# Key projection by seven block products with summed context blocks, in a one-core perceiver block

## The chip, the cores and the metric

The kernel runs on one NeuronCore of a Trainium2 chip. The metric is the device time of one execution in microseconds (us), lower being better; for the kernel before it is 1882.07 us, the median of three runs. A profile is one further execution recorded by the hardware profiler.

The engines are TensorE (PE; its weight loads are shown apart as PEld), VectorE (DVE), ScalarE (ACT), GpSimd (POOL) and SyncE (SP). Each works through its own instructions in the order in which the program issues them and waits for the others by semaphores. SP only issues DMAs here. A matrix product reads its operands from SBUF and writes into one of eight PSUM banks (128 partitions x 512 fp32 each), and DVE or ACT must take the result from there.

## The reference, cut to what matters

```python
def xattn(query, key, value, Wq, Wk, Wv, Wo):      # 32 query heads, 8 key heads of 32
    q = (query @ Wq).reshape(b, sq, 32, 32).transpose(0, 2, 1, 3)
    k = (key @ Wk).reshape(b, sk, 8, 32).transpose(0, 2, 1, 3)
    v = (value @ Wv).reshape(b, sk, 8, 32).transpose(0, 2, 1, 3)
    k, v = repeat(k, 4, axis=1), repeat(v, 4, axis=1)
    probs = softmax(einsum('bhqd,bhkd->bhqk', q, k) * 32 ** -0.5)
    return einsum('bhqk,bhkd->bhqd', probs, v).transpose(0, 2, 1, 3).reshape(b, sq, 1024) @ Wo

x = x + xattn(layernorm(x), ctx_4096, ctx_4096, Wq, Wk, Wv, Wo)
x = x + self_attention_with_rope(layernorm(x), ...)
x = x + quantised_ffn(layernorm(x), ...)
```

`x` is 16 x 64 x 1024, the context 16 x 1024 x 1024, all fp32. Each of the 16 batches has 64 queries and 1024 context rows; `Wk` and `Wv` are 1024 x 256. The projection of the context to keys and values is the largest product of the program. The other two layers work on the 1024 rows of `x` alone.

## The kernel before, in words

**Memory.** Nearly all of SBUF is one tile, `arena`, and `place(kb, shape)` gives a view at a fixed address in it. A `Ring` hands out several addresses in turn: `kv_ring` holds keys and values of batches, `stream` two halves of a context (2 MB each, 512 rows), `p_ring` seven score tiles of 8 KB per partition. So in the profile most operands are called `arena`, and lines tell them apart.

**Start.** The first context half is projected while it arrives (`project_first`, L353 and L361). Queries of all batches are computed by `query` (through L226) and kept in SBUF in `queries`. The attention outputs of all batches later take the same places (`outputs`).

**The unit loop.** `for n in range(2 * B)` (L955) goes over 32 units: a unit is one batch `b = n // 2` and one group `g = n % 2` of four key heads. In each turn, four steps i = 0 to 3 mix three units. The scores of the *following* unit come from `by_key(i)`: 16 PE instructions (L452) into two PSUM tiles, which ACT copies to SBUF (L464) while DVE takes the running maximum over the keys (L468, L471). After i = 3 the maxima are reduced over the partitions by DVE (`reduce`, L476 to L483), sent through HBM and spread to all partitions by two small DMAs of SP (`spread`, L489 and L490). The *present* unit goes through `exponentials`: DVE subtracts the maxima (L495), ACT takes the exponential (L496), POOL adds up the denominators (L499, L502); two of the four in i = 1, two in i = 2. Then `values` multiplies by the values on PE (L511): two of four key blocks in i = 2, two in i = 3. The *last* unit is ended in i = 0 by `finish`: PE sums the denominators over the partitions (L521), DVE inverts and multiplies (L528 to L535), POOL copies a half (L538).

**Fillers.** Between these, `fill()` puts pieces of the projection of batch b + 1 on PE, twice in each i, so eight in a turn and sixteen in a batch. `project` (L315) makes them: per context half, keys for two column groups of 128 (two pieces each of four calls, 512 columns, through `matmul_steps`, whose product stands at L226) and four `values` pieces (eight calls of 256 columns, L333). ACT copies each result to SBUF (L327, L340). A call of an fp32 product is two PE instructions in the profile. `load_context(b + 1, 1)` stands ahead of i = 0 of an even turn, `load_context(b + 2, 0)` in i = 1 of an odd one; each is one DMA of SP into the `stream` ring.

**Beside it,** ACT quantises the feed-forward weights in pieces (`treat_piece`, L399 to L407), with loads and stores by SP (L391, L408). POOL issues no DMA in this kernel.

**Order.** The whole stands under `tc.manual_schedule()`: each engine gets its instructions in the order in which the code calls them. The last batch's turns take the output projection (`project_out`) as fillers, and the other layers follow.

Of the kernel before, what the change touches and what calls it, by code (L numbers as in the profile page):

```python
# [11 lines left out]
F32 = mybir.dt.float32  # L12
# [9 lines left out]
P = 128  # L22
# [28 lines left out]
def kernel(  # L51
# [24 lines left out]
    small = ctx.enter_context(tc.tile_pool(name="small", bufs=6))  # L76
    arenap = ctx.enter_context(tc.tile_pool(name="arena", bufs=1))
    ps_t = ctx.enter_context(tc.tile_pool(name="ps_t", bufs=1, space=PSUM))
    ps_m = ctx.enter_context(tc.tile_pool(name="ps_m", bufs=2, space=PSUM))
    ps_w_closed = ExitStack()  # L80
    ps_w = ps_w_closed.enter_context(tc.tile_pool(name="ps_w", bufs=1, space=PSUM))

    turns = [0]

    def t_tile(shape, dtype, name, n=None):

        turns[0] ^= 1
        n = turns[0] if n is None else n
        return ps_t.tile(shape, dtype, tag=f"t{n}", name=name)

    def m_tile(name):
        return ps_m.tile([P, 512], F32, tag="m", name=name)


    arena = arenap.tile([P, int(ARENA * 256)], F32, name="arena")
# [57 lines left out]
    ternary_d = dram.tile([NCH, P, INTER], F8, name="ternary2")  # L153
    ternary.append([ternary_d[c] for c in range(NCH)])

    tops = [dram.tile([1, 1024], F32, name=f"tops{i}") for i in range(2)]

    def layernorm(dst, src, name):
# [20 lines left out]

    qa = [place(16 * g, [B * 4 * NQ]) for g in range(2)]
    queries = [a.rearrange("p (b r q) -> p b r q", r=4, q=NQ) for a in qa]
    outputs = [a.rearrange("p (t r b q) -> p t r b q", r=4, b=2, q=NQ) for a in qa]
    kv_ring = Ring(32, 40, 48, 56)
    stream = Ring(64, 80)

# [27 lines left out]
            engine.dma_start(st[:, i * n : (i + 1) * n], src[:, i * n : (i + 1) * n])  # L215
        return st

    def matmul_steps(out, lhsT, rhs, done):

        made = []  # L220

        def piece(first):
            if first:
                made.append(out())
            for k in range(0, 4) if first else range(4, KC):
                nc.tensor.matmul(  # L226
                    made[0], lhsT=lhsT(k), rhs=rhs(k), start=(k == 0), stop=(k == KC - 1)
                )
            if not first:
                done(made[0])  # L230

        return [lambda: piece(True), lambda: piece(False)]

# [21 lines left out]
    def transposed(dst, cols, xn, parted_at, turned_at):  # L257
# [13 lines left out]
        def join(i):  # L271
# [14 lines left out]
            n1T[t // 4],  # L286
            bass.ts(t % 4, P),
            n1s[t],
            4 * t if t < 4 else 8 + 4 * (t % 2),
            16 + 4 * t if t < 4 else 24 + 4 * (t % 2),  # L290
        )
        for t in range(NT)
# [5 lines left out]

    def query(half, g, r, xT):

        dst = queries[g][:, half * 8 : half * 8 + 8, r, :]
        return matmul_steps(
            lambda: m_tile(f"q_{half}_{g}_{r}"),
            lambda k: wqs[g][:, r, k, :],
            lambda k: xT[k // 4][:, k % 4, :],
            lambda ps: nc.scalar.mul(dst, ps.rearrange("p (b q) -> p b q", q=NQ), SCALE),
        )


# [5 lines left out]
    def project(b):  # L315


        kT = kv_ring.next([2, NK])
        v = kv_ring.next([8, KVD])
        key_steps, value_steps = [], []  # L320

        def keys(h, g):
            return matmul_steps(
                lambda: m_tile(f"k_{b}_{h}_{g}"),
                lambda k: wkvs[:, k, bass.ts(g, P)],
                lambda k: ctx_halves[b, h][:, k, :],
                lambda ps: nc.scalar.copy(kT[:, g, bass.ts(h, 512)], ps),  # L327
            )

        def values(h, kt):  # L330
            ps = m_tile(f"v_{b}_{h}_{kt}")
            for k in range(KC):
                nc.tensor.matmul(  # L333
                    ps[:, :KVD],
                    lhsT=ctx_halves[b, h][:, k, bass.ts(kt, P)],
                    rhs=wkvs[:, k, KVD:],
                    start=(k == 0),
                    stop=(k == KC - 1),
                )
            nc.scalar.copy(v[:, h * 4 + kt, :], ps[:, :KVD])  # L340

        for h in range(2):
            key_steps.append(keys(h, 0) + keys(h, 1))
            value_steps.append([lambda h=h, kt=kt: values(h, kt) for kt in range(4)])
        return kT, v, key_steps, value_steps

    def project_first(kT, v):

# [89 lines left out]
    class Unit:  # L438
# [4 lines left out]
        def by_key(self, i):  # L443

            ws = [
                ps_w.tile([P, 2, 2, 256], F32, tag=f"w{h}", name=f"t_{self.n}_{i}_{h}")
                for h in range(2)
            ]
            for a in range(2):
                for jj in range(4):  # L450
                    rows = bass.ts(jj, HD)
                    nc.tensor.matmul(  # L452
                        ws[jj // 2][:, jj % 2, a, :],
                        lhsT=self.kT[rows, self.g, bass.ts(i * 2 + a, P)],
                        rhs=qa[self.g][rows, bass.ts(self.b, 256)],
                        start=True,
                        stop=True,
                    )
            pt = p_ring.next([4, 2, 256])
            self.pts.append(pt)  # L460

            for turn in range(2):
                mine, other = turn, 1 - turn
                nc.scalar.copy(pt[:, 2 * mine : 2 * mine + 2], ws[mine])  # L464
                m = most[:, bass.ts(other, 512)].rearrange("p (j c) -> p j c", j=2)
                w = ws[other]
                if i == 0:
                    nc.vector.tensor_reduce(m, w.rearrange("p j a c -> p j c a"), AX.X, ALU.max)  # L468
                else:
                    for a in range(2):  # L470
                        nc.vector.tensor_tensor(m, w[:, :, a], m, ALU.max)  # L471
# [47 lines left out]
        def finish(self):  # L519
            for jj in range(4):  # L520
                nc.tensor.matmul(  # L521
                    self.po[bass.ts(jj, HD), 256:512],
                    lhsT=ones,
                    rhs=acc[:, jj, :],
                    start=True,
                    stop=True,
                )
            nc.vector.reciprocal(rs, self.po[:, 256:512])  # L528

            view = outputs[self.g][:, self.b // 2]  # L530
            split = lambda a: a.rearrange("p (r q) -> p r q", q=NQ)
            if self.b % 2 == 0:
                nc.vector.tensor_tensor(aside[self.g], self.po[:, 0:256], rs, ALU.mult)
            else:
                nc.vector.tensor_tensor(  # L535
                    view[:, :, 1, :], split(self.po[:, 0:256]), split(rs), ALU.mult
                )
                nc.gpsimd.tensor_copy(view[:, :, 0, :], split(aside[self.g]))  # L538
# [4 lines left out]
    def project_out(t, h):  # L543
        cols = bass.ts(h, 512)
        return matmul_steps(
            lambda: m_tile(f"wo_{t}_{h}"),
            lambda k: outputs[k // 4][:, t, k % 4, :, :],
            lambda k: wos[h][:, k, :],
            lambda ps: nc.vector.tensor_tensor(xs[t][:, cols], ps, xs[t][:, cols], ALU.add),
        )  # L550


# [357 lines left out]
    with tc.manual_schedule():  # L910
# [23 lines left out]
        for half in range(2):  # L934
            for g in range(2):
                for r in range(4):
# [10 lines left out]
                    treat_piece()  # L947
                    if half == 1 and g == 1 and r == 2:
                        unit.reduce()
        unit.spread()  # L950
        load_context(1, 0)
        fillers += value_steps[1]

        tiles = [(kT, v)]
        for n in range(2 * B):  # L955

            b = n // 2
            if n % 2 == 0:
                fill(len(fillers))
                if b + 1 < B:  # L960
                    load_context(b + 1, 1)
                    kT, v, key_steps, value_steps = project(b + 1)
                    tiles.append((kT, v))
                    for h in range(2):
                        fillers += key_steps[h] + value_steps[h]
                else:
                    for t in range(4):
                        load_x(xs[t], t)
                    nc.sync.dma_start(wkvs2, wkv2)
                    for h in range(2):  # L970
                        for t in (4, 5):
                            fillers += project_out(t, h)
                    for t in (0, 1):
                        for h in range(2):
                            fillers += project_out(t, h)
            following = Unit(n + 1, *tiles[(n + 1) // 2]) if n + 1 < 2 * B else None

            for i in range(4):
# [10 lines left out]
                if i == 1 and n % 2 == 1:  # L989
# [2 lines left out]
                        load_context(b + 2, 0)  # L992
                    elif b + 2 == B:
                        wos.append(load(wo[0]))
                fill()
                if i in (1, 2) and following:
                    unit.exponentials(2 * i - 2)
                if i == 1 and not following:
                    unit.exponentials(1)
                fill()  # L1000
                if last and i == 0:
                    last.finish()
                    if not following:
                        unit.exponentials(0)
                if i in (1, 2) and following:
                    unit.exponentials(2 * i - 1)
                if i == 1 and not following:
                    unit.exponentials(2)
                    unit.exponentials(3)
                if i > 1:  # L1010
                    unit.values((2 * i - 4, 2 * i - 3))
            if n == 2 * B - 4:
                for t in (4, 5):
                    load_x(xs[t], t)
# [7 lines left out]
        for t in (2, 3):  # L1022
# [2 lines left out]
                if t == 2:  # L1025
                    fillers += [lambda h=h: norm2(h)]
            fillers += [lambda t=t: (join2(t - 2), norm2(t))]
        fill(5)
        last.finish()
        fill(len(fillers))  # L1030
        for h in range(2):
# [181 lines left out]
```

## Time and profile before

| | |
|---|---|
| runs of the kernel | 1882.07 us median of 3 (1879.47 to 1882.31) |
| the profiled execution | 1879.54 us; span of its instructions 1877.8 us |
| mean granted PE clock | 0.999 |
| turns of the unit loop | 36.9 us each, from about 187 us on |
| two turns (713 to 787 us): busy PE, DVE, ACT, POOL | 74.0, 55.1, 49.2, 41.6 us of 74.0 |
| the same stretch: share of the DMA engines, rate | 0.38, 132 GB/s |
| a 2 MB context load, from issue to landing | 9.0 us median, 4.5 to 15.1 |
| product of 512 fp32 columns (L226, keys) | 1056 instructions, 470.0 us |

A line of a group reads: line, engine, operation, output <- input, shapes, count; behind the bar the busy time and the mean duration of one in ns; behind the second bar the time that the engine sat idle ahead of such instructions, and what ended it. Matrix products overlap in the pipeline, so the mean duration of one is longer than its share of the busy time. A line of a timeline reads: start in us, length in us, engine, line, operation, how many were merged, and in brackets an idle stretch ahead of it with its releaser. The chain of waits follows the program back from its last instruction, at each step to what released it, and gives shares of the span.

### The profile page before, as it was taken

What the parts mean: (1) busy time and instruction counts of PE and PEld (TensorE: products, weight loads), DVE (VectorE), ACT (ScalarE), POOL (GpSimd) and SP (SyncE); (2) the same over time, 40 slices, a digit from 0 to 9 for tenths busy, and PEclk for the clock granted to TensorE, in tenths of its full rate; (3) what the DMA queues carried; (4) which work ended last, traced back from release to release, by engine and by line L of the source; (5) the groups of instructions that cost most, each with busy time, mean ns of one, the idle gap of its engine ahead of it and who ended that gap; (6) DMA issues with size and microseconds to landing.
All of it is one profiled execution on the core that took longest, in us unless ns stands there. A gap on an engine that the chain in (4) does not pass through costs nothing.

```text
span 1877.8 us, 26794 instructions
## 1 busy us (share of the span) xinstructions
PE 1859.0 (99%) x11264; PEld 1089.8 (58%) x11264; DVE 1171.5 (62%) x1352; ACT 891.9 (47%) x932; POOL 840.7 (45%) x411
## 2 busy tenths in 40 slices
PE   8999999999999999999999999999999999999999
PEld 5445566566656655665666566555445464566654
DVE  3312777677777767776777777677534236566464
ACT  2433666566566665766666666544223021332110
POOL 0000466456546654664565456546702424444430
PEclk9999999999999999999999999999999999999999
DMA  9634343443352334324333423223034001134334
GB/s 331 179 104 176 101 163 132 143 177 117 114 179 95 132 124 159 131 104 149 144 113 124 176 95 132 101 99 146 35 66 118 0 2 42 27 85 120 104 77 110
DMA packets 112456, 221.74 MB, mean 118 GB/s; under 512 B 71568, under 2 KB 80720, under 8 KB 107344
## 3 DMA queue, kind: packets, MB, share of 16 engines
q1 hardware_dynamic: 111184, 217.94, 35.6%
q10 hardware_dynamic: 1152, 2.10, 0.3%
q8 instruction: 88, 1.44, 0.3%
q14 instruction: 32, 0.26, 0.0%
HBM read 190.98 MB, written 12.78 MB: 109 GB/s over the span
## 4 chain that ended last, share of the span: by engine, by line
PE 96%; DVE 2%; DMA 1%; POOL 0%; ACT 0%; issue 0%; DVEq 0%; ACTq 0%; POOLq 0%
PE k L226 24%; PE v L333 23%; PE q L226 12%; PE t L452 7%; PE o L511 6%; PE wo L226 6%; PE gu L831 4%; PE d L890 4%; PE g L831 3%; PE v L614 1%; PE o L521 1%; PE k_first L353 1%; PE w L654 1%; PE v_first L361 1%; DMA arena<-in_ctxT 0%; PE w L718 0%
## 5 line engine op out<-in xcount | busy, mean ns | idle before, releaser
L502 POOL TENSOR_TENSOR arena<-arena 128x1024 f32<-128x1024 f32 x192 | 578.4, 3012 | 15.3 <-POOL arena L499 0.2
L226 PE MATMUL k<-arena 128*128 128x512 f32 x1056 | 470.0, 598 | 0.9 <-DMA arena<-in_ctxT 0.9
L333 PE MATMUL v<-arena 128*128 128x256 f32 x1984 | 444.4, 382 | 0.0
L333 PEld LDWEIGHTS v<-arena 128*128 128x128 f32 x1984 | 372.3, 190 | 68.2 <-issue 20.4
L495 DVE TENSOR_TENSOR arena<-arena 128x2048 f32<-128x2048 f32 x128 | 366.6, 2902 | 0.0
L499 POOL TENSOR_TENSOR arena<-arena 128x1024 f32<-128x1024 f32 x32 | 77.6, 2425 | 619.8 <-ACT arena L496 593.6
L471 DVE TENSOR_TENSOR arena<-t,arena 128x512 f32<-128x512 f32 x384 | 261.4, 688 | 147.9 <-ACT arena L464 96.4
L226 PEld LDWEIGHTS k<-arena 128*128 128x128 f32 x1056 | 195.7, 190 | 243.7 <-issue 243.6
L464 ACT COPY arena<-t 128x1024 f32<-128x1024 f32 x256 | 252.0, 1010 | 167.7 <-PE t L452 111.8
L496 ACT ACTIVATE arena<-arena 128x2048 f32<-128x2048 f32 x128 | 244.7, 1912 | 177.1 <-DVE arena L495 177.1
L226 PE MATMUL q<-arena 128*128 128x512 f32 x512 | 226.1, 599 | 0.0
L226 PEld LDWEIGHTS q<-arena 128*128 128x128 f32 x512 | 96.6, 191 | 118.8 <-issue 117.3
L528 DVE RECIPROCAL arena<-o 128x256 f32<-128x256 f32 x32 | 56.2, 1756 | 151.7 <-PE o L521 151.7
L452 PE MATMUL t<-arena 32*128 32x256 f32 x2048 | 146.7, 400 | 0.0
L452 PEld LDWEIGHTS t<-arena 32*128 32x128 f32 x2048 | 92.5, 184 | 67.8 <-issue 57.7
L831 PEld LDWEIGHTS <-arena 128*128 128x128 bf16 x1024 | 98.3, 97 | 54.7 <-issue 5.4
L511 PE MATMUL o<-arena 128*32 128x256 f32 x2048 | 123.8, 382 | 0.0
L468 DVE TENSOR_REDUCE arena<-t 128x512 f32<-128x1024 f32 x64 | 75.4, 1219 | 64.3 <-PE t L452 64.3
L843 POOL TENSOR_TENSOR arena<-arena 128x344 f32<-128x344 f32 x64 | 70.8, 1109 | 98.5 <-DVE arena L840 89.0
L226 PE MATMUL wo<-arena 128*128 128x512 f32 x256 | 112.3, 596 | 0.0
L511 PEld LDWEIGHTS o<-arena 128*32 128x32 f32 x2048 | 60.1, 110 | 55.8 <-issue 21.4
L596 POOL TENSOR_TENSOR arena<-arena 128x512 f32<-128x512 f32 x20 | 35.5, 1773 | 120.1 <-DVE arena L594 120.1
(117 smaller groups left out, 1502.5 us busy)
## 6 DMA issues: line engine op xcount, KB each, us to landing
arena<-in_ctxT SPq DMA_DIRECT2D x31, 2048.0 KB, 9.0
arena<-in_wg SPq DMA_DIRECT2D x32, 688.0 KB, 4.5
arena<-in_wu SPq DMA_DIRECT2D x32, 688.0 KB, 4.3
arena<-in_wd SPq DMA_DIRECT2D x32, 688.0 KB, 4.2
arena<-tops SPq DMA_DIRECT2D x32, 512.0 KB, 4.2
arena<-ternary SPq DMA_DIRECT2D x32, 344.0 KB, 3.5
ternary<-arena SPq DMA_DIRECT2D x48, 172.0 KB, 1.9
arena<-in_x SPq DMA_DIRECT2D x16, 512.0 KB, 8.0
```

Source lines behind the costliest of these rows:

```text
L226: nc.tensor.matmul(made[0], lhsT=lhsT(k), rhs=rhs(k), start=(k == 0), stop=(k == KC - 1))
L333: nc.tensor.matmul(ps[:, :KVD], lhsT=ctx_halves[b, h][:, k, bass.ts(kt, P)], rhs=wkvs[:, k, KVD:], start=(k == 0), stop=(k == KC - 1),)
L452: nc.tensor.matmul(ws[jj // 2][:, jj % 2, a, :], lhsT=self.kT[rows, self.g, bass.ts(i * 2 + a, P)], rhs=qa[self.g][rows, bass.ts(self.b, 2 ...
L464: nc.scalar.copy(pt[:, 2 * mine : 2 * mine + 2], ws[mine])
L468: nc.vector.tensor_reduce(m, w.rearrange("p j a c -> p j c a"), AX.X, ALU.max)
L471: nc.vector.tensor_tensor(m, w[:, :, a], m, ALU.max)
L495: nc.vector.tensor_tensor(pt, pt, by.to_broadcast([P, 4, 2, 256]), ALU.subtract)
L496: nc.scalar.activation(pt, pt, AF.Exp)
L499: nc.gpsimd.tensor_tensor(acc, pt[:, :, 0], pt[:, :, 1], ALU.add)
L502: nc.gpsimd.tensor_tensor(acc, acc, pt[:, :, a], ALU.add)
L511: nc.tensor.matmul(self.po[bass.ts(jj, HD), 0:256], lhsT=self.v[:, kt, bass.ts(self.g * 4 + jj, HD)], rhs=self.pts[i][:, jj, a, :], start= ...
L831: nc.tensor.matmul(ps[:, :CW], lhsT=xqT[t][:, k, :], rhs=wbs[n][i][:, k, :], start=(k == 0), stop=(k == KC - 1),)
```

## The change

From batch 2 on, keys come from `project_fast`, and not from `project`. Write C for a context half's four 128-row blocks of the contraction: for batch b let c(h, i) be half h of the context rows, half i of the 1024 features, and B11, B21 (features) x first 128 key columns, B12, B22 the same for the last 128 columns. Ordinarily the four key blocks k11, k12, k21, k22 take eight products c(h, i) B. The new scheme takes seven, each of four calls of 512 columns, with sums of weight blocks (made once by `weight_sums`: four small DVE operations) and sums of context blocks:

- `chained` begins as c(1,0) by a plain load, then c(1,1), c(0,0) and c(0,1) are added to it in this order;
- `paired` begins as c(1,0), then c(0,0) is added.

All additions to these two are DMAs issued by POOL with `accum_op=ALU.add`, 1 MB each, from the context in HBM; both beginnings are 1 MB loads by SP. The order of the 30 filler pieces of a batch (two calls of 512 columns each, or four of 256) is p1, z5, values, p2, z6, values, z7, z4, p3, values, values; z5 reads `chained` after its first addition, z6 after its second, p3 after its third, and z7 reads `paired`. Two of the products add into PSUM banks that hold earlier ones (p2 on p1, p3 on z5). Three banks rotate over the batches. The results are combined by five DVE operations of 512 columns per batch, two of which are put off with `later` until `flush()` behind the subtractions; ACT copies two key results and four values results of 512 columns.

Fillers are now half as long, and each i takes four of them, i = 3 three. The second half of `values` goes from i = 3 to i = 0 of the next turn, ahead of `finish`. For batches 0 and 1 the old projection stays.

To make room in SBUF for `chained`, `paired` and the weight sums, queries no longer stay there: all but the first two tiles (four batches) are written to HBM (`spilled`) after the start and loaded again tile by tile, and outputs are written to HBM (`results`) every fourth turn and loaded together in turn 29 for the output projection.

The diff, cut to its core:

```diff
+    def weight_sums():
+        nc.vector.tensor_tensor(s, b11, b12, ALU.subtract)
+        nc.vector.tensor_tensor(z7, b12, b22, ALU.subtract)
+        nc.vector.tensor_tensor(t, b22, s, ALU.add)
+        nc.vector.tensor_tensor(z4, b21, t, ALU.subtract)
+    def quarter(b, h, i):
+        return ctxT[b, h, :, 4 * i : 4 * i + 4, :]
+    def begin_chain(b):
+        nc.sync.dma_start(chained, quarter(b, 1, 0))
+    def begin_pair(b):
+        nc.sync.dma_start(paired, quarter(b, 1, 0))
+    def add_to_chain(b, h, i):
+        nc.gpsimd.dma_start(chained, quarter(b, h, i), accum_op=ALU.add)
+    def add_to_pair(b):
+        nc.gpsimd.dma_start(paired, quarter(b, 0, 0), accum_op=ALU.add)
...
+    def project_fast(b):
...
+        def after_z7(ps):
+            op(k21, ps, k12, ALU.subtract)()
+            op(k22, k21, held[z_bank], ALU.subtract)()
+        steps = (
+            product("p1", x_bank, b11, lambda: whole(0, 0), lambda ps: nc.scalar.copy(k12, ps))
+            + product("z5", z_bank, s, lambda: chained, lambda ps: None)
+            + values(0, 0, y_bank)
+            + product("p2", x_bank, b21, lambda: whole(0, 1), lambda ps: nc.scalar.copy(k11, ps), first=False)
+            + product("z6", y_bank, t, lambda: chained, lambda ps: later.append(op(k12, k12, ps, ALU.subtract)))
+            + values(0, 1, x_bank)
+            + product("z7", y_bank, w7, lambda: paired, after_z7)
+            + product("z4", x_bank, w4, lambda: whole(1, 1), lambda ps: op(k21, ps, k21, ALU.add)())
+            + product("p3", z_bank, b22, lambda: chained, lambda ps: later.append(op(k12, ps, k12, ALU.add)), first=False)
+            + values(1, 0, y_bank)
+            + values(1, 1, x_bank)
+        )
...
-                        rhs=qa[self.g][rows, bass.ts(self.b, 256)],
+                        rhs=two_tiles[self.b // 2 % 2][rows, self.g, self.b % 2, :],
...
+        for t in range(4, NT):
+            nc.sync.dma_start(spilled[t], place(4 * t, [DIM]))
...
+                elif b + 1 < B:
+                    kT, v, steps = project_fast(b + 1)
+                    fillers += steps
...
+                fast, odd = 1 <= b < B - 1, n % 2
+                if i == 1 and not odd and fast:
+                    add_to_chain(b + 1, 0, 0)
+                if i == 3 and not odd and fast:
+                    add_to_chain(b + 1, 0, 1)
+                if b + 2 < B and odd:
+                    if i == 1:
+                        begin_pair(b + 2)
+                    if i == 2:
+                        begin_chain(b + 2)
+                        add_to_pair(b + 2)
+                    if i == 3:
+                        add_to_chain(b + 2, 1, 1)
...
+                if n % 4 == 0 and 0 <= t < NT - 2:
+                    if i == 1:
+                        nc.sync.dma_start(results[t], place(4 * (t % 2), [DIM]))
+                    if i == 2:
+                        nc.sync.dma_start(place(4 * (t % 2), [DIM]), spilled[t + 2])
+                if n == 2 * B - 3 and i == 2:
+                    for t in (4, 5, 0, 1, 2, 3):
+                        nc.sync.dma_start(outputs[t].rearrange("p g r c -> p (g r c)"), results[t])
-                fill()
+                fill(2)
                 if i in (1, 2) and following:
                     unit.exponentials(2 * i - 2)
+                flush()
...
-                fill()
+                fill(1 if i == 3 and fast else 2)
                 if last and i == 0:
+                    last.values((2, 3))
                     last.finish()
...
+                flush()
+                if i == 2:
+                    unit.values((0, 1))
+                if i == 3 and not following:
+                    unit.values((2, 3))
-                if i > 1:
-                    unit.values((2 * i - 4, 2 * i - 3))
```

## The prediction

> **What bounds the kernel now.** First the page's busy shares and its chain of work:
>
> ```profile
> span 1877.8 us, 26794 instructions
> ...
> PE 1859.0 (99%) x11264; PEld 1089.8 (58%) x11264; DVE 1171.5 (62%) x1352; ACT 891.9 (47%) x932; POOL 840.7 (45%) x411
> ...
> PE k L226 24%; PE v L333 23%; PE q L226 12%; PE t L452 7%; PE o L511 6%; PE wo L226 6%; PE gu L831 4%; PE d L890 4%; PE g L831 3%; PE v L614 1%; PE o L521 1%; PE k_first L353 1%; PE w L654 1%; PE v_first L361 1%; DMA arena<-in_ctxT 0%; PE w L718 0%
> ...
> L502 POOL TENSOR_TENSOR arena<-arena 128x1024 f32<-128x1024 f32 x192 | 578.4, 3012 | 15.3 <-POOL arena L499 0.2
> L226 PE MATMUL k<-arena 128*128 128x512 f32 x1056 | 470.0, 598 | 0.9 <-DMA arena<-in_ctxT 0.9
> ```
>
> TensorE sets the end: 96% of the chain, and the key products alone 24%. A key matmul occupies PE for 470.0 / 1056 = 0.445 us (the 598 ns include the pipeline), and one call in the code is two such instructions, 0.89 us. So removed calls are worth time, as long as PE still waits for nobody. That needs the second view: the timeline of one turn of the unit loop (n odd or even, i = 0 to 3).
>
> ```profile
> 703.68 0.64 PE L521 MATMUL o<-arena,ones 128*32 128x256 f32 x8
> 704.25 1.15 PE L452 MATMUL t<-arena 32*128 32x256 f32 x16
> 705.32 7.13 PE L226 MATMUL k<-arena 128*128 128x512 f32 x16
> ...
> 712.38 1.15 PE L452 MATMUL t<-arena 32*128 32x256 f32 x16
> ...
> 713.52 2.38 POOL L499 TENSOR_TENSOR arena<-arena 128x1024 f32<-128x1024 f32 x1 [16.01 <-ACT arena L496]
> ...
> 716.10 18.46 POOL L502 TENSOR_TENSOR arena<-arena 128x1024 f32<-128x1024 f32 x6 [0.21 <-POOL arena L499]
> ...
> 722.43 1.15 PE L452 MATMUL t<-arena 32*128 32x256 f32 x16
> ...
> 727.89 1.42 DVE L471 TENSOR_TENSOR arena<-t,arena 128x512 f32<-128x512 f32 x2 [1.55 <-ACT arena L464]
> ...
> 732.47 1.15 PE L452 MATMUL t<-arena 32*128 32x256 f32 x16
> ```
>
> The four `t` lines start i = 1, 2, 3 and the next turn's i = 0. I count from the start of i = 1 (704.25). i = 2 comes at +8.13, i = 3 at +18.18, the next i = 0 at +28.22; i = 0 lasts 8.7 (consecutive i = 1 are 36.93 apart, the period). DVE has read the last scores of i = 3 at +25.06 (727.89 + 1.42), 3.2 us ahead of the next `t`. POOL's seven softmax sums start at +9.27 and end at **+30.31** (734.56), so 2 us into the next turn. Their only reader, L521, comes 6 us later: today POOL's lateness is free.
>
> **The change, part by part.** All costs are per batch (two turns), and 14 of 16 batches change.
>
> Removed: keys take 7 products of 4 calls instead of 32 calls, so 4 calls x 2 x 0.445 = **-3.56 us** on PE. If nothing waits, that is 14 x 3.56 = 49.8 us.
>
> Moved: the second half of `values` (1.9 us, 720.57 to 722.43 is one such half) goes from i = 3 to i = 0 of the next turn, and i = 3 gets three half-size pieces, not four. So i = 3 shrinks from 10.04 to 1.08 + 3 x 1.77 = 6.37, i = 0 grows to 10.6, and the next i = 0 now falls at +24.55. The `values` half itself costs nothing: its exponentials are 6 us older there.
>
> Added, DVE: five combinations of 512 columns at the 0.69 us of L471. In the even turn the one after z6 lies in the 1.55 us that DVE waits for ACT at 727.89, so it is hidden, as is that after p3 behind a like wait in i = 2. Those after z7 fall in i = 0, where DVE idles 5.25 us ahead of the reciprocal. Only the one after z4 stands ahead of the subtractions of i = 1, where DVE runs on end: it moves everything on DVE, ACT and POOL by 0.69. The cover of 3.2 us at the next `t` is gone, since that comes 3.67 earlier: `t` gets the two score banks at +25.06 and so waits **0.5 us** in an even turn, and at +25.75 with the shift, **1.2 us**, in an odd one. ACT loses copies (8 of 0.37 and 4 of 0.58 become 4 + 2 of 0.58): off the path.
>
> Added, POOL: four accumulating DMAs per batch stand in POOL's order between softmax sums. This is the heart of it. In the odd turn the program has sums 0 and 1, pair += c00, sums 2 and 3, and then chain += c11 at i = 3. POOL reaches the last at +30.31 + 0.69 + G, G being what one issue occupies of POOL. Then it must be issued (G) and land (D). But z5, the second product of the next batch, multiplies the chain at 25.75 + 1.08 + 3.53 = +30.36. So PE waits 31.0 + 2G + D - 30.36 = **0.6 + 2G + D**. Behind the waiting z5 on PE are all of i = 0, the `finish` and the next `t`, and DVE, ACT and POOL restart only from these (at 9.27 after i = 1), so the wait returns in every batch and nothing recovers it.
>
> G: no DMA of this trace is issued by POOL. Below: SP's issue of a 2 MB load, 0.38 us; above: one POOL sum, 3.0. I take 0.67, POOL's small operation L177, the nearest to a short job on that engine. D: no accumulating DMA either.
>
> ```profile
> arena<-in_ctxT SPq DMA_DIRECT2D x31, 2048.0 KB, 9.0
> arena<-in_wg SPq DMA_DIRECT2D x32, 688.0 KB, 4.5
> ```
>
> Below: a plain 1 MB would take 4.5 + 336/1360 x 4.5 = 5.6. Above: the longest landing of a context load, 15.1, as the next 2 MB context load leaves SP right after the row maxima come back (734.49, +30.2), on top of this transfer. I take **9.0**, the 2 MB row, because each added MB is read twice over (source and destination). So z5 waits 0.6 + 1.3 + 9.0 = **10.9 us**.
>
> The Trainium skill, "DMA: Bandwidth & Descriptors", section "Anatomy of one DMA — SWDGE (gpsimd) path", fits a DMA of POOL with 2.0 us plus bytes over 436 GB/s: 4.4 us for 1 MB, which says nothing of accumulation; by it z5 would wait 6.3 and the total below would be some 70 us less. The rows of 4.5 us for 688 KB here are slower than that fit (3.6), so I stay with the rows.
>
> The same in the even turn for p3, with less harm: chain += c01 is issued at +30.24 + G and lands D later, and p3 stands at 25.05 + 10.6 + 1.08 + 1.77 = +38.5. It waits 30.24 + 0.67 + 9.0 - 38.5 = **1.4 us**. (chain += c00 is issued when z5 ends and has 15.6 us until z6; pair is ready half a turn before z7.)
>
> PE after an idle stretch:
>
> ```profile
> 5.46 3.78 PE L353 MATMUL k_first<-arena 128*128 128x512 f32 x4 [5.46 <-DMA arena<-in_wkv]
> ...
> 11.33 1.88 PE L353 MATMUL k_first<-arena 128*128 128x512 f32 x4
> ```
>
> The first four matmuls after 5.46 us of idleness took 3.78, later ones 1.88. The granted clock of that stretch reads 1.00, so the rows leave it between 0 and **+1.9 us** for each long wait; I take 1.9, since single matmuls there are twice as long (1102 ns on the mean) and not only spaced out. The Trainium skill, "TensorE: Matmul & The Clock Gate", section "Part 1: The HAM clock gate (the "warmup" mystery)", has TensorE at half clock after an idle window of 3.4 us until it was busy for one: it speaks against any change that idles PE, and would make the cost 1.7 us.
>
> Queries and outputs through HBM: some 12 MB in 24 transfers of 512 KB on SP over 1100 us, beside 4 MB of context per batch; SP's load into a tile waits for the store from it, with nothing due within a turn behind it. DMA engines are busy 37% of this stage. Nothing.
>
> Sum per batch: -3.56 + 0.5 + 1.2 + 10.9 + 1.4 + 1.9 = **+12.3 us**; times 14 = +173. The profiled execution took 1879.54 us (span 1877.8), 2.5 under the median of 1882.07 and within the runs shown. 1879.5 + 173 = **2052 us**.
>
> **The rivals.** *Faster: POOL's issue overtakes its arithmetic.* If an accumulation leaves as soon as its own data are there and the sums before it are merely dispatched, chain += c11 leaves when the last exponential is ready (DVE 724.93 plus an ACT exponential of 1.91, +22.6, plus 0.69) and lands with D = 5.6 before z5. Then only 0.5 + 1.2 remain: -1.86 x 14 = -26, **1853 us**; it decides once 2G + D counted from there is under 8 us. Against it: the sums run on POOL back to back for 20.8 us, and L538, queued behind them, starts only at their end (734.51). *Much slower: D is 15.1*, accumulation and the context load sharing the engines in full: z5 waits 17.0, p3 7.5 with a second slow start: +26.4 x 14 = +370, **2249**. *Little change:* D about 4 with G about 0.3 and no slow start: z5 waits 5.2, +3.3 x 14, 1926; for about no change z5 may wait only 1.9, less than any load of this size takes in the trace.
>
> **How the numbers follow.** The forecast's mechanism 0.75 (with D from 5.6 to 13: 1949 to some 2200), the slow case 0.13, faster 0.10, within 0.2% 0.02 (0.2% is about what a measurement tells from no change). All unknowns at their low ends (G 0.38, D 5.6, no slow start) give z5 7.0, +5.1 x 14, 1951; all at the high ends (G 3.0, D 15.1) +33 x 14, 2350. The range 1930 to 2200 leaves out the fast case and most of the slow one.
>
> **What would show it.** Right: PE idle ahead of z5 in each even turn, put down to a DMA into the arena, 5 to 17 us long; POOL's issue standing right behind L502's sums; small PE waits for DVE or ACT ahead of `t`. Wrong: z5 without a wait, a POOL issue before the sums end, or `t` waits much longer than 1.2 us; 1853 or less would mean that the order on POOL doesn't bind.

## The result, and the profile after

The changed kernel takes 2092.44 us (median of four runs, 2072.14 to 2095.33) against 1882.07: a ratio of 1.1098, with a 95% interval of 1.1028 to 1.1169. The forecast was 2052 us, in a range of 1930 to 2200. The profiled execution took 2093.23 us. From its page (line numbers are now those of the changed kernel: L425 is the product of a block scheme, L586 the scores, L636 POOL's sums, L395 an addition to the chain):

```profile
span 2091.5 us, 26778 instructions
...
PE 1860.1 (89%) x11152; PEld 1085.9 (52%) x11152; DVE 1214.8 (58%) x1426; ACT 873.0 (42%) x848; POOL 871.3 (42%) x467
...
PE 46%; DVE 18%; POOL 15%; DMA 10%; ACT 7%; issue 4%; POOLq 0%; SPq 0%; ACTq 0%; DVEq 0%
...
L425 PE MATMUL z<-arena 128*128 128x512 f32 x560 | 292.7, 669 | 191.9 <-DMA arena<-in_ctxT 142.7
...
L395 POOL DMA_DIRECT2D arena<-in_ctxT x42 | 36.8, 877 | 211.8 <-PE z L425 211.8
...
arena<-in_ctxT SPq DMA_DIRECT2D x31, 2048.0 KB, 12.7
arena<-in_ctxT POOLq DMA_DIRECT2D x56, 1024.0 KB, 10.4
```

PE has 112 instructions fewer (11152 for 11264), as the scheme says, and yet is not less busy (1860.1 us for 1859.0). It is idle for 231.4 us where it was idle for 18.8, and PE's share of the chain fell from 96% to 46%: the chain now runs through POOL's sums and the DMAs, back to DVE and ACT. Two views of the timeline show where, first PE and POOL, then SP:

```profile
789.34 1.15 PE L586 MATMUL t<-arena 32*128 32x256 f32 x16 [0.96 <-DVE arena L605]
790.42 3.70 PE L425 MATMUL p<-arena 128*128 128x512 f32 x8
805.56 6.10 PE L425 MATMUL z<-arena 128*128 128x512 f32 x8 [11.44 <-DMA arena<-in_ctxT]
...
848.21 3.54 PE L425 MATMUL z<-arena 128*128 128x512 f32 x4 [2.82 <-ACT arena L452]
```

```profile
783.30 11.14 POOL L636 TENSOR_TENSOR arena<-arena 128x1024 f32<-128x1024 f32 x4
794.39 0.87 POOL L395 DMA_DIRECT2D arena<-in_ctxT  x1
```

```profile
793.03 0.32 SPq L623 DMA_DIRECT2D tops<-arena  x1
797.70 0.33 SPq L624 DMA_DIRECT2D arena<-tops  x1
798.12 0.68 SPq L225 DMA_DIRECT2D arena<-in_ctxT  x1
```

The even turn begins at 789.34. p1 runs, and then z5 (805.56) waits 11.44 us. What it waits for left POOL at 794.39, in the instant in which the softmax sums ended (783.30 + 11.14 = 794.44), and landed 11.1 us later; z5 started 0.05 us after that. In all 14 batches z5 starts within 0.1 us of the landing. The 2 MB context load went out beside it at 798.12. After the wait, eight matmuls take 6.10 us and not 3.60. A wait that the prediction did not have stands at 848.21: z4, 2.82 us, for ACT's copy of a values result (L452). ACT's order ahead of the same wait one batch earlier, where z4 starts at 756.47 (L598 copies scores, L537 and L541 quantise weights):

```profile
748.42 1.01 ACT L598 COPY arena<-t 128x1024 f32<-128x1024 f32 x1 [1.91 <-PE t L586]
752.03 1.01 ACT L598 COPY arena<-t 128x1024 f32<-128x1024 f32 x1 [2.59 <-DVE arena L602]
752.94 1.53 ACT L537 ACTIVATE arena<-arena,magic,inverse 128x1376 f32<-128x1376 f32 x1
754.50 1.44 ACT L541 ACTIVATE arena<-arena,magic 128x1376 fp8e4<-128x1376 f32 x1
755.85 0.57 ACT L452 COPY arena<-v 128x512 f32<-128x512 f32 x1
```

The whole difference of the spans divides into three parts: 56 calls saved at two instructions each, -49.8; slower matmuls, +50.9 (busy time 1860.1 - 1859.0 + 49.8); more idle time, +212.6; together 213.7 = 2091.5 - 1877.8.

### The profile page after: what moved, and what is told of

Same layout as the page of the kernel before. It is cut to its first block, busy times and chain, and to the rows that moved or that the text cites. A ratio compares the mean times of both kernels' runs of the same rounds, so it can differ in the third digit from the quotient of the medians.

```text
span 2091.5 us, 26778 instructions
## 1 busy us (share of the span) xinstructions
PE 1860.1 (89%) x11152; PEld 1085.9 (52%) x11152; DVE 1214.8 (58%) x1426; ACT 873.0 (42%) x848; POOL 871.3 (42%) x467
## 3 DMA queue, kind: packets, MB, share of 16 engines
q0 software_dynamic: 8064, 58.72, 14.7%
## 4 chain that ended last, share of the span: by engine, by line
PE 46%; DVE 18%; POOL 15%; DMA 10%; ACT 7%; issue 4%; POOLq 0%; SPq 0%; ACTq 0%; DVEq 0%
POOL arena L636 13%; PE q L243 11%; DMA arena<-in_ctxT 9%; DVE arena L629 7%; PE z L425 6%; PE wo L243 5%; DVE arena L605 4%; PE d L1025 4%; PE gu L966 4%; ACT arena L630 3%; PE g L966 3%; PE o L645 3%; PE k L243 3%; DVE arena L662 2%; POOL arena L633 2%
## 5 line engine op out<-in xcount | busy, mean ns | idle before, releaser
L636 POOL TENSOR_TENSOR arena<-arena 128x1024 f32<-128x1024 f32 x192 | 565.8, 2947 | 18.3 <-ACT arena L630 4.4
L425 PE MATMUL z<-arena 128*128 128x512 f32 x560 | 292.7, 669 | 191.9 <-DMA arena<-in_ctxT 142.7
L598 ACT COPY arena<-t 128x1024 f32<-128x1024 f32 x256 | 252.6, 1010 | 466.9 <-PE t L586 359.3
L444 PE MATMUL v<-arena 128*128 128x256 f32 x1792 | 407.8, 383 | 0.0
L444 PEld LDWEIGHTS v<-arena 128*128 128x128 f32 x1792 | 334.7, 190 | 71.9 <-issue 29.6
L633 POOL TENSOR_TENSOR arena<-arena 128x1024 f32<-128x1024 f32 x32 | 77.5, 2421 | 576.4 <-ACT arena L630 559.6
L425 PEld LDWEIGHTS z<-arena 128*128 128x128 f32 x560 | 115.5, 214 | 348.7 <-DMA arena<-in_ctxT 146.7
L586 PE MATMUL t<-arena 32*128 32x256 f32 x2048 | 146.6, 400 | 16.6 <-DVE arena L605 14.6
L586 PEld LDWEIGHTS t<-arena 32*128 32x128 f32 x2048 | 93.7, 184 | 70.6 <-issue 40.9
L395 POOL DMA_DIRECT2D arena<-in_ctxT x42 | 36.8, 877 | 211.8 <-PE z L425 211.8
L425 PE MATMUL p<-arena 128*128 128x512 f32 x224 | 103.6, 605 | 0.0
## 6 DMA issues: line engine op xcount, KB each, us to landing
arena<-in_ctxT POOLq DMA_DIRECT2D x56, 1024.0 KB, 10.4
arena<-in_ctxT SPq DMA_DIRECT2D x28, 1024.0 KB, 10.5
```

The source lines that it names most:

```text
L425: nc.tensor.matmul(held[n], lhsT=weights[:, k, :], rhs=what()[:, k, :], start=(first and k == 0), stop=(k == 3), skip_group_check=not first,)
L444: nc.tensor.matmul(held[n][:, bass.ts(kt, KVD)], lhsT=ctx_halves[b, h][:, k, bass.ts(2 * pair + kt, P)], rhs=wkvs[:, k, KVD:], start=(k == 0),
L586: nc.tensor.matmul(ws[jj // 2][:, jj % 2, a, :], lhsT=self.kT[rows, self.g, bass.ts(i * 2 + a, P)], rhs=two_tiles[self.b // 2 % 2][rows, s ...
L633: nc.gpsimd.tensor_tensor(acc, pt[:, :, 0], pt[:, :, 1], ALU.add)
L636: nc.gpsimd.tensor_tensor(acc, acc, pt[:, :, a], ALU.add)
```

## The experiments

**No summed blocks.** z5, z6, z7 and p3 read ordinary blocks; the scheme's products, its DVE combinations, bank changes and the order stay.

```diff
-            + product("z5", z_bank, s, lambda: chained, lambda ps: None)
+            + product("z5", z_bank, s, lambda: whole(0, 0), lambda ps: None)
...
-                if b + 2 < B and odd:
-                    if i == 1:
-                        begin_pair(b + 2)
-                    if i == 2:
-                        begin_chain(b + 2)
-                        add_to_pair(b + 2)
-                    if i == 3:
-                        add_to_chain(b + 2, 1, 1)
```

> Leaves out all loads and additions of the summed context blocks; z5, z6, z7 and p3 read plain context blocks, so keys from batch 2 on are not the reference's. All PE, DVE and ACT work stays. Theory (the loss is PE waiting for the sums' transfers): the waits of z5 (151.6 us in all), the slow restarts after them (about 30) and of p3 (about 8) go, the waits of t (17) and of z4 for ACT (33) stay: some 1900 us. Rival (the scheme costs on the engines: three rotating banks, DVE combinations, shorter fillers): it stays above 2000.

Measured: 1898.55 us, ratio to the kernel before 1.0095 (1.0071 to 1.0120). From its page:

```profile
span 1898.4 us, 26574 instructions
...
PE 1824.8 (96%) x11152; PEld 1074.4 (57%) x11152; DVE 1215.3 (64%) x1426; ACT 871.7 (46%) x848; POOL 839.5 (44%) x411
```

The loss is thus in the transfers, all but 18 us of it. But these 18 us matter too: in this order, even sums that cost nothing would have left a loss, though the scheme saves 49.8 us of PE. In this trace t still waits about 20 us (some 1 us in each even turn, some 0.4 in each odd one) and z4 2.8 us per batch from turn 9 on (1.2 before, 31.6 in all).

**Plain transfers on the same queue.**

```diff
-        nc.gpsimd.dma_start(chained, quarter(b, h, i), accum_op=ALU.add)
+        nc.gpsimd.dma_start(chained, quarter(b, h, i))
...
-        nc.gpsimd.dma_start(paired, quarter(b, 0, 0), accum_op=ALU.add)
+        nc.gpsimd.dma_start(paired, quarter(b, 0, 0))
```

> The four additions per batch become plain loads from the same queue at the same places, so keys are not the reference's. Theory as forecast (each added MB is read twice): a 1 MB transfer of POOL lands in 6 to 7 us in place of 10.4, z5 waits about 7 in place of 10.8, and with the restarts unchanged the time falls by about 50 us to some 2040. Rival (landing is set by sharing the engines with the 2 MB context load sent at the same moment): 10 us again, and the time within 15 us of the changed kernel.

Measured: 2037.72 us (ratio 1.0836, 1.0801 to 1.0871). Its DMA issues:

```profile
arena<-in_ctxT SPq DMA_DIRECT2D x31, 2048.0 KB, 11.2
arena<-in_ctxT POOLq DMA_DIRECT2D x56, 1024.0 KB, 6.9
arena<-in_ctxT SPq DMA_DIRECT2D x28, 1024.0 KB, 10.5
```

The third column is KB, the fourth the median time to landing: 6.9 us in place of 10.4 at the same place and on the same queue. So an accumulating MB takes 3.5 us more than a plain one, and that is worth 55 us of the 210. POOL's queue moves the same bytes in both, yet its packets fill twice the share of the DMA engines' time; first the changed kernel, then this run (packets, MB, share of 16 engines):

```profile
q0 software_dynamic: 8064, 58.72, 14.7%
```

```profile
q0 software_dynamic: 8064, 58.72, 7.6%
```

The remaining waits of z5 (92.1 + 9.9 us in the view of waits, for 151.6) are there with plain transfers as well: the place in POOL's order.

**The chain's beginning and its second transfer earlier.** The beginning now stands behind the fillers of i = 1.

```diff
                     if i == 2:
-                        begin_chain(b + 2)
+                        add_to_chain(b + 2, 1, 1)
                         add_to_pair(b + 2)
-                    if i == 3:
-                        add_to_chain(b + 2, 1, 1)
...
+                if b + 2 < B and odd and i == 1:
+                    begin_chain(b + 2)
```

> Only the second transfer of the chain is moved: its plain beginning to the end of i = 1 of the odd turn, right behind p3, and chain += c11 ahead of sums 2 and 3 on POOL, in i = 2. Same work. Theory (the place in POOL's order, and of the beginning in SP's, makes z5 wait): c11 is added by +30, z5 doesn't wait or waits under 2 us, and the time falls by 150 to 185 us to about 1905 to 1940. Rival (the transfers are too slow or too many wherever they stand): z5 keeps a wait of 5 us or more, over 1990.

Measured: 1934.89 us (1.0294, 1.0266 to 1.0321). The view of PE's waits, first of the changed kernel, then of this one (total us, times, longest):

```profile
PE z L425 <- DMA arena<-in_ctxT: 142.7, 16, 15.4
PE z L425 <- ACT arena L452: 31.6, 13, 2.8
PE z L425 <- issue: 15.6, 1, 15.6
PE t L586 <- DVE arena L605: 14.6, 19, 1.2
```

```profile
PE t L586 <- DVE arena L605: 28.2, 19, 3.4
PE z L425 <- ACT arena L452: 22.9, 14, 2.8
PE t L586 <- ACT arena L598: 17.8, 6, 3.4
...
PE z L425 <- DMA arena<-in_ctxT: 5.1, 3, 3.3
```

Same transfers, same bytes, 10.6 us to landing in the median, and z's waits for them fall from 158.3 (with the one labelled issue) to 5.1; the three that are left are p3's, and z5 has none. The edit moves the beginning of the chain as well, in SP's order. But in the changed kernel's trace the beginning had landed 3.9 us or more before c11 left POOL, in all 14 batches, so it was not what held c11. This shows that POOL's order made z5 wait. In place of z5, t now waits, 46 us in all, for the score banks.

**The ACT piece behind z4's bank copy.** As the run before, and in i = 0 of odd turns `treat_piece` is called behind the first two fillers.

> As the run before, and in i = 0 of odd turns the weight piece of ACT stands behind the first two fillers, so the copy of the values result comes ahead of it. Theory (z4 waits 2.8 us for its bank, whose copy stands behind 3 us of weight quantisation on ACT): the waits of z4 go but for about 0.5, 30 to 40 us less than the run before, so 1865 to 1905. Rival (z4's bank copy is late because ACT must first copy the scores, whose second copy waits for DVE): less than 15 us gained.

Measured: 1919.62 us (1.0200, 1.0169 to 1.0232), 15 us less than the run before, not 30 to 40, which is the upper border of the rival's case. The waits of z4 for ACT are gone from the timeline, as the theory says, so the copy did stand behind the weight piece. But p3 now reaches the chain earlier and waits for the context in its place in most batches (up to 3.2 us): z4's waits for ACT were some 19 us before, and p3's grew by about 10.

**Ordinary keys with the rest of the change.**

```diff
-                    kT, v, steps = project_fast(b + 1)
-                    fillers += steps
+                    kT, v, key_steps, value_steps = project(b + 1)
...
-                fill(1 if i == 3 and fast else 2)
+                fill(2)
```

> The changed kernel with ordinary keys in every batch (32 calls) and no summed blocks; what stays of the change is queries and outputs through HBM, the later half of the values products and the finer spacing. Theory (these cost nothing; the forecast priced them at 0): within 6 us of the kernel before, 1876 to 1888. Rival (the HBM round trips or the moved values product make part of the loss): 1895 or more.

Measured: 1881.91 us, ratio 1.0010 (1.0000 to 1.0019). By the interval, queries and outputs in HBM and the moved values product together cost at most some 3.6 us. About finer fillers this run says nothing, though its expectation counts them in: `project` makes pieces of the old size, each followed by an empty one.

**Another order of the products, without the summed blocks.** Three fillers in i = 0 and four in i = 3; the order is p1, values, z5, p2, values, z6, z7, z4, values, p3, values; z6 and the second values result exchange banks, z4's combination is put off behind a subtraction and z6's no longer is, POOL's sums 1 move into i = 2, and weight pieces stand behind the first two fillers.

> Seven products without the summed blocks' transfers (z5, z6, z7 and p3 read plain blocks, so keys are not the reference's), with the fillers in another order: three pieces in i = 0 and four in i = 3, z6 and z7 in banks whose readers are long done, ACT's weight pieces behind the first two fillers. Theory (what the run without sums still lost to waits of t and z4, about 50 us with its slow restarts, is a matter of order): these waits go and the saved products show, 1840 to 1860. Rival (the five DVE combinations and the bank changes cost PE wherever they stand): above 1875.

Measured: 1834.07 us, ratio 0.9757 (0.9741 to 0.9773), better than expected. Its keys are not the reference's, so this is no kernel to use.

```profile
span 1830.7 us, 26595 instructions
...
PE 1806.8 (99%) x11152; PEld 1072.3 (59%) x11152; DVE 1216.5 (66%) x1426; ACT 872.5 (48%) x848; POOL 848.4 (46%) x411
```

PE is busy 99% again, with 52 us less busy time. Against the kernel before in the same set of runs (1879.68) the seven products deliver 45.6 of their 49.8 us; so DVE's five combinations, the three banks and the finer fillers cost little when they are placed well. Order, banks and ACT's pieces were changed together here, and what each is worth was not tried.

**The same order with the summed blocks.** The chain begins behind p3, c11 goes ahead of sums 3, c00 ahead of sums 1, c01 out in the odd turn's i = 0, the pair ahead of sums 2. In turn 29 the outputs are loaded over the chain ahead of p3, so the keys of batch 15 are not the reference's.

> The run before with the summed blocks again, so that the keys are right: the beginning of the chain behind p3, c11 ahead of sums 3, c00 ahead of sums 1 of the even turn, c01 at the start of the odd turn, the pair ahead of sums 2. Each product that reads a sum stands 11 us or more behind the issue of its addition. Theory (the loss was the place of the transfers, not the transfers): waits of z5, z6, p3 under 1 us, 1850 to 1885. Rival (the transfers, 10 us each in the changed kernel, load the DMA engines so that the row maxima or the weights come late): 1900 to 1925, with DVE waiting for the maxima.

Measured: 1895.70 us (1.0086, 1.0068 to 1.0105), between the two expectations and nearer the rival's. Where the sums stand is no longer the matter (PE waits 4.9 us in all for them), yet the blocks' transfers cost 61 us against the same order without them, and t waits 34 us in place of 2. From 526 to 1220 us the DMA engines are now busy 0.74 of the time, and 0.40 in the run before. Small transfers come late: the maxima's store and load together take 10.5 us at the start of even turns and took 5.5, a 172 KB weight store 5.1 and took 2.7 (medians). A view of SP and ACT in the timeline:

```profile
696.95 0.33 SPq L620 DMA_DIRECT2D tops<-arena  x1
703.36 0.33 SPq L621 DMA_DIRECT2D arena<-tops  x1
...
708.00 1.44 ACT L538 ACTIVATE arena<-arena,magic 128x1376 fp8e4<-128x1376 f32 x1 [6.98 <-DMA ternary<-arena]
```

The 4 KB store of the row maxima lands 6.4 us after its issue, so the load that spreads them is late; and ACT, ahead of a score copy, waits 6.98 us for a store of weights to land.

**c11 some 3 us later, meant to leave behind the store of the maxima.** c11 goes between the two additions of sums 3, and the outputs' load behind p3.

> As the reordered run, but chain += c11 stands between the two additions of sums 3 on POOL, some 3 us later, and the outputs are loaded again after p3 of the last turns (in the reordered run they were loaded ahead of it, so keys of batch 15 were not the reference's there; here they are). Theory (what is left of the loss is the row maxima: their 4 KB store lands 6.4 us after its issue, not 1.4, because two additions are in flight, so DVE starts the even turn late and PE waits for the score banks): with the addition behind the store, the store lands in under 2.5 us, the waits of t fall by about 20 us, and the time to 1865 to 1885. Rival (a later addition only trades this for waits of z5, and the engines of DMA are simply too full): 1890 to 1910, with waits of z5 for the context of 2 us or more in most batches.

Measured: 1891.40 us (1.0066, 1.0035 to 1.0097), a time of the rival's, but without its waits of z5. The same stretch as above:

```profile
694.95 0.32 SPq L620 DMA_DIRECT2D tops<-arena  x1
696.32 0.33 SPq L621 DMA_DIRECT2D arena<-tops  x1
...
704.73 1.44 ACT L538 ACTIVATE arena<-arena,magic 128x1376 fp8e4<-128x1376 f32 x1 [5.71 <-DMA ternary<-arena]
```

Here the store lands in 1.4 us, but this batch is an exception. In 11 of the 14 even turns that follow an addition c11 still left POOL about 1.1 us ahead of the store, and the store took 6.2 to 7.1 us; the median in the run before was 6.2. Where c11 left only 0.1 to 0.4 us ahead, the store took 1.3 to 1.4 us (3.6 once), but the load that spreads the maxima took 6.8 to 9.1 us in place of some 4: store and load together stay at 10.5 us in the median. So the edit did not make the maxima early, and the waits of t, 36 us in all, say nothing for or against them. The third line shows another cause: ACT waits 5.71 us for the weight store before it, and the score copies stand behind.

**Weight pieces further apart**, and then **the last of them out of the way of the score copies.**

```diff
-                due = n < 8 or i % 2 == 0 and (n, i) != (8, 0) or i == 3 and n % 2 == 1
+                due = n < 8 or i in ((1, 2), (0, 2, 3))[n % 2] and (n, i) != (8, 1)
+                at_end = due and 8 < n < 28 and (n % 2, i) in ((0, 2), (1, 3))
...
-                due = n < 8 or i in ((1, 2), (0, 2, 3))[n % 2] and (n, i) != (8, 1)
-                at_end = due and 8 < n < 28 and (n % 2, i) in ((0, 2), (1, 3))
+                due = n < 8 or i in ((1, 3), (0, 2, 3))[n % 2] and (n, i) != (8, 1)
+                at_end = due and 8 < n < 28 and (n % 2, i) == (1, 3)
```

> As the run before, with only the weight pieces of ACT at other places (odd turns i = 0, i = 2 and the end of i = 3, even turns i = 1 and the end of i = 2; before: i = 0 and 2 of both and i = 3 of odd ones). Theory (what still makes t wait is that the second of two weight pieces 8 us apart waits 5.7 us on ACT for the store of the first, which lands in 5.4 us in place of 1.9 because the summed blocks fill the DMA engines; ACT's score copies stand behind it): the waits of t fall from 36 us to under 15, and the time to 1855 to 1872, below both kernels. Rival (DVE and POOL, not ACT, make the even turn late): the waits of t stay at 30 us or more, 1880 to 1895.

Measured: 1881.46 us (1.0021, 1.0011 to 1.0031), not the 1855 to 1872 expected. The waits of about 1 us inside even turns (ahead of i = 2) are gone from turn 9 on, as the theory has it. But the wait at the start of odd turns, 2.2 to 2.5 us in the run before, stays, at 2.6 to 2.8: there the moved piece now stands ahead of the score copies. The waits of t sum to 29 us, not under 15.

> As the run before, but ACT's second weight piece of an even turn stands in i = 3 behind the first two fillers, not at the end of i = 2. Theory (the 2.6 us that t still waits at the start of every odd turn from turn 11 to 27 come from that piece, 3 us of ACT ahead of the score copies of i = 3): these nine waits fall under 1 us, and with their slow restarts 20 to 35 us go: 1848 to 1864, below both kernels by more than 0.8%. Rival (DVE is the late one there, by its five combinations and POOL's contention, and the piece only hides it): the waits stay above 2 us and the time above 1872.

Measured: **1867.40 us**, ratio 0.9938 (0.9916 to 0.9960): 0.6% below the kernel before, and far below the changed kernel. The expectation of 1848 to 1864, more than 0.8% below, was a little low. Nine waits of 2.6 us are gone. What is left, from PE's timeline:

```profile
815.00 2.09 PE L583 MATMUL t<-arena 32*128 32x256 f32 x16 [4.86 <-DVE arena L460]
...
1178.04 1.89 PE L583 MATMUL t<-arena 32*128 32x256 f32 x16 [5.06 <-DVE arena L460]
```

Two waits of some 5 us for a late combination, and smaller ones. In both, DVE had itself waited 5.0 to 5.2 us for a score copy, and ACT ahead of that copy 8.0 to 8.2 us for a weight store. The maxima still take 10.3 us to come back here, so late maxima alone need not hold PE. Against the run without the summed blocks 33 us are left. Its runs spread from 1857.79 to 1881.95, those of the kernel before from 1877.86 to 1883.73. Why they spread more was not tried.

## Why the prediction was right, and where it was off

| step of the sum | forecast, us | measured in the trace, us |
|---|---|---|
| calls removed | -49.8 | -49.8 |
| z5 waits for chain += c11, 14 times | 14 x 10.9 = +153 | +151.6 (8.5 to 15.6 each) |
| t waits for the score banks | 14 x 1.7 = +24 | +17 |
| p3 waits for chain += c01 | 14 x 1.4 = +20 | +9 |
| slower matmuls after waits | 14 x 1.9 = +27 | +51 |
| z4 waits for its bank | none | +32 |
| sum | +173 | +213.7, some 3 in small waits |

**The mechanism** was right and is shown: POOL issues c11 as the sums end, 30.7 us after the start of i = 1 in the stretch shown (forecast 31.0 + G = 31.7), PE waits in every even turn for it, and moving the chain's transfers ahead in that order takes the wait away. The rival in which POOL's issue overtakes its arithmetic fell: 794.39 is the end of the sums to 0.1 us.

**Issue and landing.** G was 0.87 us as a row, with the next operation 0.6 after its start (forecast 0.67), D 10.4 us in the median of all additions and 10.7 on the mean of c11 alone (9.0). The reason given for 9.0, that an added MB is read twice, fits the 10.4 against 6.9 of a plain one and the doubled share of the DMA engines' time; that reading the destination is what doubles it is an inference, the two differences are shown. z5's wait came out at 10.8 on the mean, for a forecast of 10.9. That it agrees so closely is luck: POOL issued c11 1.3 us earlier on the mean, set against PE's arrival at z5, than forecast, and the second G of 0.7 us is part of the landing time as the trace counts it, while the landing took 1.7 us more. Single waits lie between 8.5 and 15.6 us. One sum of the prediction is off: a wait of z5 of 6.3 us, from a D of 4.4, makes the total 84 us less by its own terms (4.6 for z5 and 1.4 for p3, 14 times), not some 70.

**Queries and outputs in HBM, and the moved values product at nothing**: shown by the run with ordinary keys, to within 3.6 us.

**The step that failed** is the one on ACT: "ACT loses copies (8 of 0.37 and 4 of 0.58 become 4 + 2 of 0.58): off the path." ACT has less to do, but z4 takes the bank of the values result just ahead of z7, and the copy that frees it stands in ACT's order behind two score copies and, from turn 9 on, behind 3 us of weight quantisation. z4 waits 2.8 us per batch there and 1.2 before, and the missed 32 us with their slow restarts are most of the 40 us by which the forecast was low. The prediction counted ACT's time and not ACT's order.

**The slow restarts** were priced too low: eight matmuls after z5's wait took 5.75 us on the mean and not 3.60, 2.15 more (forecast 1.9). That is 30 of the 51 us lost in all; some 7 lie in the first four matmuls behind z4's waits, and the rest was not divided further. The windows of the changed kernel (us, then PE, PEld, DVE, ACT, POOL; the clock is the seventh value):

```profile
705.00:714.00 9.00, 0.00 (x0) 0.00 (x0) 0.00 (x0) 2.58 (x3) 0.00 (x0) 0.67 1.00 259
714.00:720.00 6.00, 5.80 (x12) 2.39 (x16) 0.00 (x0) 0.00 (x0) 0.00 (x0) 0.65 0.89 363
720.00:731.00 11.00, 11.00 (x100) 8.43 (x96) 8.63 (x8) 3.67 (x3) 0.86 (x1) 1.00 0.65 149
...
756.00:761.00 5.00, 4.53 (x12) 1.58 (x16) 0.00 (x0) 0.42 (x1) 0.00 (x0) 0.50 1.05 221
```

The granted clock reads 0.67 over the wait and 0.65 over the six us behind it. The last line is the stretch behind z4's wait of 2.77 us: 0.50. The Trainium skill, "TensorE: Matmul & The Clock Gate", section "Part 1: The HAM clock gate (the "warmup" mystery)", has half clock after an idle window of about 3.4 us; here it followed a shorter wait too, in four of ten such waits of z4 (the next four matmuls took 3.5 to 3.8 us, else 1.98).

**p3's wait** was forecast at 1.4 us and appears only in the first three batches and the last (1.4 to 3.3 us): in the others z4's wait of 2.8 us holds PE back so that c01 has time to land, and where the fourth run takes z4's waits away, p3's come back.

**Without z5's wait** the fast rival had 1853 us, with only the waits of t left. The run without the blocks' transfers took 1898.55: t's waits of 20 us it had, but not z4's 32 us, nor matmuls 16 us slower in all (PE busy 1824.8 us, where 1859.0 - 49.8 = 1809.2 were due). Until the order is changed these eat more than the scheme saves.

## What to carry to other kernels

A DMA that POOL issued left here when POOL's earlier work was done, not when its own data were ready: where a compute engine issues a transfer, work out the time at which the engine reaches it, add the landing (for an accumulating 1 MB here 10.4 us), and only then look at the reader. When an engine at 99% loses work, look next at the order on the engines that free its buffers, not at their busy share: even without the transfers all of the gain of 49.8 us was lost to waits for banks not yet read out and to slow matmuls behind them, and 45.6 us came back by another order of products, banks and ACT's pieces. And transfers can cost though the DMA engines have time left (busy 0.74 of the loop here): they make small ones late, and the engine that waits for these is late too.

## What the runs showed of the hardware

- An accumulating 1 MB transfer takes 10.4 us to land where a plain one on the same queue takes 6.9, and its packets fill the DMA engines for twice the time (14.7% and 7.6% of the span).
- POOL is occupied by an issue for 0.6 us to the next operation's start, and its issues keep their place behind its arithmetic.
- PE's granted clock can fall after a wait of only 2.8 us, not each time (0.50 over the five us behind one; four of ten such waits in the changed kernel); the waits of 8.5 to 15.6 us cost a further 2.15 us on the mean in the next eight matmuls.
- A 4 KB store takes 1.3 to 1.4 us to land, and 6.2 to 7.1 where an accumulating MB left about 1.1 us ahead of it; where the MB left 0.1 to 0.4 us ahead, the store took 1.3, 1.4 and 3.6 us, and the load that spreads its 4 KB to all partitions was the late one (6.8 to 9.1 us in place of some 4).
- A 172 KB store lands in 2.7 us (median) without the summed blocks' transfers and in 5.1 with them, in the same order of the program; in the kernel before it took 1.9.
